# Two-layer decoder with selective scans: convolution taps made by TensorE from diagonals, and a 3 MB load placed behind row loads

## The chip, the core and the metric

The kernel runs on one core of a Trainium2 chip. A core has five engines that run their own instruction queues in order and meet through semaphores: TensorE (PE; its weight loads are listed as PEld), VectorE (DVE), ScalarE (ACT), GpSimd (POOL) and SyncE (SP). DMAs are issued here from the queues of SP and ACT. On-chip data lies in SBUF (128 partitions); matmuls write to PSUM. The metric is the device time of one execution in microseconds (us), lower is better. One execution is also profiled; the times within the kernel are from that one.

## The reference

The input `x` is 4 batches of 256 tokens by 256 channels; `ctx_1024` is 4 x 256 x 128. Six steps follow one another, each added to `x`:

```
x = x + L0_attn(layernorm(x))                 # 8 heads of 32, 2 kv heads, window of 64
x = x + L0_xattn(ctx, z=layernorm(x))         # selective scan over ctx, gated by z
x = x + L0_ffn(layernorm(x))                  # 704 wide
x = x + L1_attn(layernorm(x))                 # 16 heads of 128, 4 kv heads, causal
x = x + L1_xattn(ctx, z=layernorm(x))         # selective scan again, other weights
x = x + L1_ffn(layernorm(x))                  # 32 experts, 6 per token, and a shared one
```

The selective scan, cut to what matters (256 inner channels `e`, 16 states `n`, 4 taps):

```
x  = in_proj_w @ ctx                          # 256 x 128
xc = causal depthwise conv(x, conv_w)         # 4 taps per channel
u  = silu(xc + conv_b)
dt_low, B, C = split(x_proj_w @ u)
dt = softplus(dt_proj_w @ dt_low + dt_proj_b)
state = state * exp(dt * A) + (dt * u) * B    # per token, channel and state
y = sum over n of state * C + D * u;  result = y * silu(z)
```

The scan reads only `ctx`, so it doesn't depend on `x`; the gate does.

## The kernel before

All arithmetic is in fp32, with few exceptions. `x` stays in SBUF. The work is one long program for all four batches; a scheduler in the language's layer decides, at build time, in which order each engine issues its instructions, from the order of the program text, the dependences and a cost model. At run time that order is fixed on each engine.

**The folded convolution.** Projection and convolution are one: for each tap `k`, `taps[:, k, :]` is `in_proj_w` (transposed, 128 x 256) times tap `k` of each channel, and four matmuls per half of the channels (L165), each on `ctx` shifted by one token, add up in PSUM. `taps` must hold the tap of channel `e` in column `e` on all 128 partitions. To get that, the kernel before copies `conv_w` from `params` to a row `cw` in device memory (L287, four loads in elements of 4 bytes, two for each layer), then broadcasts `cw` to all partitions (L290, issued on ACT's queue) and multiplies by `inproj` (L294; on DVE for layer 0, on POOL for layer 1). The tiles `inproj`, `taps`, `xproj` and `dtproj` are shared by both layers.

**The scan.** `mamba_front(l, bp, pool)` makes `u`, `dt`, `du` and writes the rows of B and C to device memory (`bc`, L180) for two batches at a time. `mamba_scan` then runs over the states: for each state and half of the channels it broadcasts one row of B (`bt`) and one of C (`ct`) to all partitions (L208, 256 KB each, on SP's queue, three buffers each), ACT makes `h` (L214), POOL makes `db` (L216), DVE scans (L217) and multiplies by `ct` into `hc` (L219); `hc` is added up by PE (L234) or POOL (L236). It is a generator: `run(s00, 4)` takes it four steps on (two states a step), so that scan and attention are interleaved in the program text.

**The first attention.** `head0(b)` normalizes and transposes a batch (L135, L139, L142), projects it (L337) and applies the rotation (`r`, `rr`, L347, L348) and the normalization with its rsqrt steps (L103 to L110) on DVE, up to `qn`, `krep` and `vn`; `tail0(b)` does scores, softmax and output and adds to `x` (L479). `far` (L319) is made of the constants `cst`. The order in the text: the front of the first two batches, `head0(0)`, `head0(1)`, and then for each `b`: four steps of scan `s00`, `head0(b + 2)`, `tail0(b)`, two more steps; after `tail0(0)` the front of the other two batches.

**The second attention's projections.** `wqkv1` (3 MB) is loaded on SP's queue (L492) after that block. For the layer norm of the queries and keys the mean of each head is taken out of the weights: `wmean` by a reduction and a scaling on DVE (L498, L499), then two subtractions on POOL (L501). Nothing holds these in their place but the data, so the scheduler puts the load right behind the first loads, and `wmean` and the subtractions before the first scan.

Then come the first FFN (gates, L530 to L562, with the rest of the scan and the fronts of layer 1), the second attention with the layer 1 scans, and the experts.

## Time and profile before

| | |
|---|---|
| median of 5 runs | 962.02 us (954.41 to 966.72) |
| the profiled execution | 963.15 us, its span 961.3 us |
| mean granted TensorE clock | 0.923 |
| busy, share of the span | PE 85%, DVE 68%, ACT 50%, POOL 53%, PEld 53% |
| HBM read | 71.58 MB, 76 GB/s over the span |
| first convolution matmul | at 30.75 us |
| first scan | at 60.45 us |
| first addition of attention to `x` | at 111.50 us |
| experts, PE full | from about 720 us to the end |

How to read it: the span runs from the first to the last instruction of the profiled execution; its own time has a few us around that. A line of a timeline gives start, duration, engine, line of the program, operation, output and inputs, a count, and in brackets how long the engine was idle before and what ended that. `SPq` and `ACTq` are the queues in which DMAs are issued. PEclk is the clock granted to TensorE, in tenths or as a share of full speed; a matmul of fp32 operands has two records.

### The profile page before, as it was taken

The numbers are of one execution on the slowest core, as the hardware profiler recorded it, in microseconds if no ns is written. First come the engines' busy times: TensorE is split into PE (matmuls) and PEld (weight loads), VectorE is DVE, ScalarE is ACT, GpSimd is POOL, SyncE is SP. The second block draws the span as 40 slices with busy tenths as digits, with TensorE's granted clock in tenths as the row PEclk, the third lists the DMA queues.
The fourth block names the chain that finished last, engine by engine and source line by source line (L and its number), as shares of the span: only waits on it lengthen the run. The fifth ranks groups of instructions, "written<-read, shape, count | busy, mean of one in ns | idle before, by whom it ended". The sixth has DMA issues, their size and how long they took to land. (4 is left out here: it accounts for less than half of the span.)

```text
span 961.3 us, 10234 instructions
## 1 busy us (share of the span) xinstructions
PE 821.5 (85%) x2986; PEld 508.9 (53%) x2986; DVE 650.0 (68%) x1230; ACT 481.1 (50%) x1187; POOL 505.9 (53%) x493
## 2 busy tenths in 40 slices
PE   0649799996996979879887988897879999999997
PEld 0226466752442435545554656465556666666665
DVE  1499976647886739998779989796225555555554
ACT  1345676647968826746684776557433111111110
POOL 2175656638667753885756698383123333333334
PEclk9979878957995979989989999899979999999999
DMA  7245443636561220121111112000030101111101
GB/s 199 110 148 163 120 152 124 207 91 214 191 200 44 76 99 1 55 77 34 55 33 55 45 48 76 10 12 1 0 111 1 44 23 45 26 40 45 44 0 44
DMA packets 38071, 73.54 MB, mean 77 GB/s; under 512 B 6512, under 2 KB 9472, under 8 KB 37760
## 3 DMA queue, kind: packets, MB, share of 16 engines
q1 hardware_dynamic: 36016, 69.92, 22.9%
q10 hardware_dynamic: 2000, 2.99, 0.9%
q8 instruction: 23, 0.38, 0.2%
q14 instruction: 32, 0.26, 0.1%
HBM read 71.58 MB, written 1.32 MB: 76 GB/s over the span
## 5 line engine op out<-in xcount | busy, mean ns | idle before, releaser
L216 POOL TENSOR_TENSOR db<-bt,du 128x512 f32<-128x512 f32 x128 | 163.8, 1289 | 80.8 <-DVE h L217 67.8
L980 DVE SCALAR_TENSOR_TENSOR acc<-ps,gate,acc 128x256 f32<-128x256 f32 x256 | 111.3, 479 | 109.3 <-PE ps L971 109.3
L217 DVE TENSOR_TENSOR_SCAN h<-h,db 128x512 f32<-128x512 f32 x128 | 153.3, 1215 | 20.1 <-ACT h L214 16.5
L945 POOL TENSOR_TENSOR hT<-hr 128x512 f32<-128x512 f32 x68 | 70.8, 1042 | 166.5 <-ACT hr L943 166.5
L943 ACT ACTIVATE hr<-ph 128x512 f32<-128x512 f32 x68 | 40.6, 598 | 181.6 <-PE ph L935 179.4
L971 PE MATMUL ps<-w,hT 128*128 128x256 f32 x512 | 120.6, 379 | 0.0
L935 PE MATMUL ph<-moe_xnT,w 128*128 128x512 f32 x256 | 120.1, 592 | 0.0
L971 PEld LDWEIGHTS ps<-w,hT 128*128 128x128 f32 x512 | 97.3, 190 | 39.7 <-issue 29.7
L619 PE MATMUL ps<-wqkv,xnT 128*128 128x512 f32 x192 | 102.8, 654 | 11.8 <-ACT sq L634 5.3
L214 ACT ACTIVATE h<-dt,negA 128x512 f32<-128x512 f32 x128 | 86.3, 688 | 52.5 <-DVE hc L219 50.1
L219 DVE TENSOR_TENSOR hc<-h,ct 128x512 f32<-128x512 f32 x128 | 85.2, 680 | 2.2
L226 POOL TENSOR_TENSOR y<-y,hc 128x512 f32<-128x512 f32 x64 | 83.1, 1305 | 5.3 <-DVE hc L219 5.1
L612 POOL TENSOR_TENSOR rq<-rq,nhalf 128x8 f32<-128x8 f32 x20 | 35.5, 1775 | 62.4 <-DVE rq L611 62.4
L746 POOL TENSOR_TENSOR sc<-sc,rsum 128x512 f32<-128x512 f32 (+1 forms) x32 | 46.6, 1476 | 41.2 <-DVE rsum L744 40.9
L935 PEld LDWEIGHTS ph<-moe_xnT,w 128*128 128x128 f32 x256 | 48.6, 190 | 34.3 <-issue 31.1
L741 ACT ACTIVATE sc<-sc,nm 128x128 f32<-128x128 f32 (+1 forms) x128 | 56.8, 450 | 17.2 <-DVE nm L736 14.7
L634 ACT ACTIVATE sq<-ps 128x128 f32<-128x128 f32 x160 | 42.7, 281 | 36.9 <-PE ps L619 33.3
L619 PEld LDWEIGHTS ps<-wqkv,xnT 128*128 128x128 f32 x192 | 36.5, 208 | 42.1 <-issue 28.2
L784 PE MATMUL ps<-wo,oT 128*128 128x256 f32 x256 | 57.0, 381 | 1.1 <-ACT oT L777 1.1
L234 PE MATMUL ps<-hc,ident 128*128 128x512 f32 x64 | 41.9, 744 | 17.1 <-DVE hc L219 17.1
L784 PEld LDWEIGHTS ps<-wo,oT 128*128 128x128 f32 x256 | 48.1, 190 | 9.7 <-ACT oT L777 3.3
L165 PE MATMUL ps<-ctxT,taps 128*128 128x512 f32 x64 | 36.9, 696 | 11.4 <-DVE taps L294 11.4
(198 smaller groups left out, 1524.8 us busy)
## 6 DMA issues: line engine op xcount, KB each, us to landing
bt<-bc SPq DMA_DIRECT2D x96, 256.0 KB, 3.3
ct<-bc SPq DMA_DIRECT2D x96, 256.0 KB, 3.5
w<-in_w_dram SPq DMA_DIRECT2D x16, 512.0 KB, 3.6
wqkv<-in_wqkv_dram SPq DMA_DIRECT2D x1, 3072.0 KB, 14.8
wo<-in_wo_dram SPq DMA_DIRECT2D x1, 2048.0 KB, 7.6
x<-in_x_dram SPq DMA_DIRECT2D x4, 256.0 KB, 5.0
taps<-cw ACTq DMA_DIRECT2D x2, 512.0 KB, 9.2
out_dram<-acc SPq DMA_DIRECT2D x4, 256.0 KB, 2.2
```

Source lines behind the costliest of these rows:

```text
L214: nc.scalar.activation(h, dt[:, c, :], AF.Exp, scale=negA[:, a : a + 1])
L216: nc.gpsimd.tensor_mul(db, bt, du[:, c, :])
L217: nc.vector.tensor_tensor_scan(h, h, db, 0.0, ALU.mult, ALU.add)
L219: nc.vector.tensor_mul(hc, h, ct)
L226: nc.gpsimd.tensor_add(y[:, c, :], y[:, c, :], state(n, c, bt, ct))
L619: mm(pq, lhsT=xnT[:, f, c * P : (c + 1) * P], rhs=wqkv1[:, f, ch * 512 : (ch + 1) * 512], start=(f == 0), stop=(f == 1),)
L741: nc.scalar.activation(part, part, AF.Exp, bias=nm[:, qc, j : j + 1], accum_out=rsum[:, qc, j : j + 1])
L784: mm(pout[:, c * 256 : (c + 1) * 256], lhsT=oTs[h // 4][:, h % 4, c * P : (c + 1) * P], rhs=wo1[:, 8 * gp + h, :], start=(h == 0), stop=(h ...
L935: mm(ph_, lhsT=w1[:, f, :], rhs=xnT[:, f, hf * 512 : (hf + 1) * 512], start=(f == 0), stop=(f == 1),)
L945: nc.gpsimd.tensor_mul(hT, hr, hr)
L971: mm(po[:, t * 256 : (t + 1) * 256], lhsT=hT[:, tl * P : (tl + 1) * P], rhs=w2, start=True, stop=True,)
L980: nc.vector.scalar_tensor_tensor(acc[:, tl, :], po[:, t * 256 : (t + 1) * 256], gate[:, tl, e : e + 1], acc[:, tl, :], ALU.mult, ALU.add,)
```

## The change

The taps are made on chip. `conv_taps(l)` multiplies the identity by the tap columns of `params` (`par`, already in SBUF, one value per partition, tap and half) into four times two 128 x 128 diagonals `diag`; a matmul with a matrix of ones then yields, on every partition, the row of taps (two matmuls of 512 columns); DVE multiplies each from PSUM by `inproj`. For layer 0 it is called ahead of the first front, for layer 1 at the start of the first FFN. The loads of `cw`, its copies in device memory and the broadcasts go; `inproj`, `taps`, `xproj` and `dtproj` now have one tile for each layer, so that layer 1's loads needn't wait for layer 0's use. PSUM for the matmuls comes from the pool `pf`, one buffer, that the fronts use as well.

The load of `wqkv1` moves into the loop, behind the first batch's steps, and is held on SP's queue behind the last row load traced so far (the `ct` of state 12, first half of the channels). This is an order of issue, not a wait for that row to land. `wmean` and the subtractions follow in the text as before; what they read lands later.

The rest of the text is the same. In the built order of instructions the engines differ from before up to the middle of the first FFN, and from there to the end they are the same; ACT's order has 62 table loads where before it had 70.

```diff
@@ mamba_scan
-            nc.sync.dma_start(out=t_, in_=bc[r : r + 1, :].to_broadcast([P, 512]))
+            loads.append(nc.sync.dma_start(out=t_, in_=bc[r : r + 1, :].to_broadcast([P, 512])).ins)
@@ per layer l
-        inproj = mp.tile([P, 256], F32, name="inproj")
-        taps = mp.tile([P, 4, 256], F32, name="taps")
-        xproj = mp.tile([P, 2, 40], F32, name="xproj")
-        dtproj = mp.tile([8, 256], F32, name="dtproj")
+        inproj = mp.tile([P, 256], F32, name=f"inproj{l}")
+        xproj = mp.tile([P, 2, 40], F32, name=f"xproj{l}")
+        dtproj = mp.tile([8, 256], F32, name=f"dtproj{l}")
         nc.scalar.dma_start(out=inproj, in_=i_)
-        cw = dpool.tile([1, 8 * P], F32, name=f"cw{l}")
-        for c in range(2):
-            w = l * M_COLS + M_CONVW + 4 * c
-            nc.sync.dma_start(
-                out=cw.rearrange("o (k c p) -> (o p) c k", k=4, c=2)[:, c, :], in_=params[:, w : w + 4]
-            )
-        nc.scalar.dma_start(out=taps.rearrange("p k e -> p (k e)"), in_=cw.to_broadcast([P, 8 * P]))
         nc.scalar.dma_start(out=xproj, in_=x_)
         nc.scalar.dma_start(out=dtproj, in_=d_)
-        (nc.vector if l == 0 else nc.gpsimd).tensor_mul(
-            taps, taps, inproj.unsqueeze(1).to_broadcast([P, 4, 256])
-        )
-        mw.append((taps, xproj, dtproj))
+        mw.append([inproj, xproj, dtproj])
+    ones = mp.tile([P, P], F32, name="ones")
+    nc.gpsimd.memset(ones, 1.0)
+    def conv_taps(l):
+        diag = mp.tile([P, 4, 2, P], F32, tag="diag", name="diag")
+        taps = mp.tile([P, 4, 256], F32, name=f"taps{l}")
+        w = par[:, l * M_COLS + M_CONVW : l * M_COLS + M_CONVW + 8].rearrange("p (c k) -> p k c", k=4)
+        nc.vector.tensor_mul(
+            diag,
+            ident.unsqueeze(1).unsqueeze(1).to_broadcast([P, 4, 2, P]),
+            w.unsqueeze(3).to_broadcast([P, 4, 2, P]),
+        )
+        for k in range(0, 4, 2):
+            pw = ps(pf)
+            mm(pw, lhsT=ones, rhs=diag[:, k : k + 2].rearrange("p k c e -> p (k c e)"), start=True, stop=True)
+            nc.vector.tensor_mul(
+                taps[:, k : k + 2, :],
+                pw.rearrange("p (k e) -> p k e", k=2),
+                mw[l][0].unsqueeze(1).to_broadcast([P, 2, 256]),
+            )
+        mw[l][0] = taps
@@ first attention
+        conv_taps(0)
         s00 = mamba_scan(mamba_front(0, 0, pf), psd, psy)
         parts = [head0(0), head0(1)]
         for b in range(B):
...
             run(s00, 2)
-    nc.sync.dma_start(out=wqkv1, in_=wqkv1_in)
+            if b == 0:
+                with tc.issue_after(loads[-1]):
+                    nc.sync.dma_start(out=wqkv1, in_=wqkv1_in)
@@ first FFN
+        conv_taps(1)
         scans = []
```

## The prediction

> **What bounds the kernel now.** I read first the busy shares in 40 slices, then the waits of the first 62 us, then that stretch in order of time, then busy time by stage. The slices (24.0 us each) show where no engine is busy:

> ```profile
> PE   0649799996996979879887988897879999999997
> DVE  1499976647886739998779989796225555555554
> POOL 2175656638667753885756698383123333333334
> PEclk9979878957995979989989999899979999999999
> ```

> The first slice is empty on all engines. From slice 30 on PE is full (the experts); before that the bound changes by stage. Who waited in the first 62 us:

> ```profile
> POOL wqkv L501 <- DVE wmean L499: 31.5, 1, 31.5
> DVE taps L294 <- DMA taps<-cw: 14.9, 1, 14.9
> PE ps L165 <- DVE taps L294: 11.4, 1, 11.4
> ACT xn L135 <- issue: 9.1, 1, 9.1
> ```

> So the first convolution waits for `taps`, and `taps` for a load. In order of time:

> ```profile
> 3.48 5.02 SPq L287 DMA_DIRECT2D cw<-in_params_dram  x4
> 16.32 0.34 ACTq L290 DMA_DIRECT2D taps<-cw  x1
> 17.50 0.60 ACT L135 ACTIVATE xn<-x,ln_nb,ln_rs 128x256 f32<-128x256 f32 x1 [9.15 <-issue]
> 29.47 1.22 DVE L294 TENSOR_TENSOR taps<-taps,inproj 128x1024 f32<-128x1024 f32 x1 [14.87 <-DMA taps<-cw]
> 30.75 5.80 PE L165 MATMUL ps<-ctxT,taps 128*128 128x512 f32 x8 [11.42 <-DVE taps L294]
> 37.87 0.49 DVE L347 TENSOR_TENSOR r<-ps,cst 128x320 f32<-128x320 f32 x1 [7.18 <-PE ps L337]
> 38.68 5.48 DVE L498 TENSOR_REDUCE wmean<-wqkv 128x40 f32<-128x5120 f32 x1
> 45.12 10.15 POOL L501 TENSOR_TENSOR wqkv<-wqkv,wmean 128x2560 f32<-128x2560 f32 x2 [31.54 <-DVE wmean L499]
> 46.90 4.05 DVE L361 SCALAR_TENSOR_TENSOR r<-a_mean,r 128x768 f32<-128x768 f32 x1
> 50.87 4.95 DVE L192 TENSOR_TENSOR du<-dt,u 128x512 f32<-128x512 f32 x1
> 60.45 1.22 DVE L217 TENSOR_TENSOR_SCAN h<-h,db 128x512 f32<-128x512 f32 x1
> ```

> The 4-byte loads of `cw` land at 16.3; only then can ACT's queue issue the broadcast of `taps`, with `xn` behind it, and that lands at 29.4, beside the 3 MB of `wqkv1` issued at 14.19. Then `wmean` and its subtraction stand ahead of the first scan (L217). By stage:

> ```profile
> core 0: us, PE busy (x) PEld busy (x) DVE busy (x) ACT busy (x) POOL busy (x), PEclk, DMA share, GB/s
> 60.45:111.50 51.05, 40.74 (x172) 24.26 (x170) 49.42 (x87) 31.74 (x60) 30.09 (x27) 0.93 0.48 146
> 111.50:217.10 105.60, 102.15 (x392) 67.14 (x393) 70.72 (x111) 65.35 (x123) 58.85 (x53) 0.76 0.44 141
> 217.10:300.00 82.90, 63.15 (x168) 28.54 (x166) 62.63 (x107) 64.20 (x79) 57.54 (x68) 0.86 0.53 175
> ```

> From the first scan to the first attention result added to `x` (111.5) DVE is full; from there to the fourth (217.1) PE is, at a granted clock of 0.76; then ACT leads with 77%, PE and DVE a point or two below it.

> **The head.** Gone are four `cw` loads, the broadcast and its wait. New for layer 0: `diag` (one 128x1024 multiply, 1.22 by the old `taps` row), two fp32 128x512 matmuls (two records each; eight took 5.80 at the first convolution, so 1.45 a matmul) and two multiplies from PSUM (0.68, the DVE rows of 128x512). `par` lands at 6.4 (issued 1.41, 5.0 to landing); DVE is free of the layer norm's sums at 9.6, so `diag` ends at 10.8, the first matmul at 12.3, the first multiply near 13. In the changed kernel's instruction order PE does the transposes of `xn` before the second matmul. `xn` needs POOL's power (ends 13.58 before; nothing here moves that), so two `xn` end at 14.8, transposes at 15.4, second matmul 16.9, second multiply 17.6. The first projection follows the second matmul (two records, 1.45): `r` at 18.4 against 37.87, 19.5 earlier; the convolution at 18.4 against 30.75, 12.3 earlier. `xn`'s 9.15 us of waiting behind the DMA goes; what is late next is that power on POOL.

> **From there to the first scan.** `wmean` (5.48 + 0.17) and what the two DVE rows above took over the same rows later (4.05 - 0.95 and 4.95 - 0.68, together 7.37) leave: 13.0. Not all counts, for the chain convolution, `u`, `xdbl`, `bc`, first row takes as long as before: from 30.75 to 50.0 (47.0 issued, 3.0 to landing) 19.3. 18.4 + 19.3 + 1.3 (`db`) = 39.0, against 60.45: 21.4. By then DVE has also finished the first head's rsqrt, `qn` and the next `r`, some 3.3 us which before came after the first scan, and DVE is full from there to 111.5. I take **25** at the first addition to `x`. Bounds: 12.3 (the convolution's start alone) and 32.5 (19.5 + 13.0).

> **What is paid back.** The load is issued behind the row `ct` of state 12, and in the changed order `wmean` stands just after the first addition to `x`, its scaling nine scans later, the two subtractions on POOL beside that.
> - `wmean`, 5.65 on DVE. It now lies where DVE is busy 67%: 3.8. Bounds 0 and 5.65.
> - The subtractions, 10.15 on POOL. POOL has three `db` made ahead when it comes to them, so `db` is covered; DVE's two-operand work behind them is not. Before, they held DVE 7.37: I take 7.4. Bounds 0 and 10.15.
> - 3 MB beside row loads, which now queue behind it on SP. The nearest row: 2.3 MB of FFN weights issued from 215.4 to 217.2, and row loads issued from 217.24 on landed within 5.3 us against 3.3. Three row buffers at 3.9 us a scan (51.05 over 13) hide that; 1. Bounds 0 and 11.5 (14.8 landing, less 3.3). DVE reaches `wmean` some 27 us after the load's slot by the times of before (91.0 to 118.1), so it should have landed.
> - The second layer's taps: 2 matmuls, 2 multiplies; its `diag` lies in the head while DVE waits. Gone: a POOL multiply of 2.35 that waited 4.61. 0; bounds -2 and 3.

> Together 12.2.

> **ACT tables.** The changed ACT stream has eight table loads fewer (1.28 each), five of them after the last attention of layer 0, where ACT is busy 77%: 6.4 x 0.77 = 5 gained. Bounds 0 and 10.2. From the second half of the FFN on the order of all engines is as before, so what is won at 300 us stays.

> Sum: -25 + 12.2 - 5 = -17.8. The profiled execution took 963.15 (span 961.3 and 1.85 around it): **945**. That execution is 1.1 above the median of 962.02.

> [...] While the subtractions ran, one DVE multiply took 4.95 instead of 0.68. [...]

> **Rivals.**
> - *The payback is hidden.* Where PE is full at 111 to 217, DVE and POOL have room: nothing paid but 1, and all tables gained: -25 + 1 - 10.2 = -34, 929. For it: DVE 67%, POOL 56%. Against it: DVE issues in order, and attention waits on it.
> - *It is paid in full.* 5.65 + 10.15 + 7.37, and no tables: -25 + 23.2 = -2, 961. For it: that is what these steps cost before.
> - *The clock falls (slower).* 111.5 to 217.1 holds 102.15 us of PE at 0.76, 77.6 at full clock. New gaps on PE while DVE does `wmean` may keep it at half clock as from 188.6 to 212.5. At a mean of 0.55 the stage takes 141, 35 more: -17.8 + 35.5 = +18, 981. It decides below 0.65 (119.4, +14).
> - *The head isn't freed.* `far`, ahead of the first multiply on DVE, waits for `cst`, which landed at 13.9; if x and `cst` come later still, only the 12.3 remains, less 12.2: no change, 963.

> **Chances.** Forecast 0.45 (its own range 935 to 953), hidden 0.18, in full 0.20, clock 0.12, head 0.05. A measurement of this kernel tells about 1% (9.6 us; its five runs spread from 954.41 to 966.72). Faster: 0.18, 0.43 of the forecast, and 0.09 of the middle cases: 0.70. Slower: the clock case, 0.11. Within: 0.19. The range leaves out the clock case and the far end of the hidden one: 929 to 965.

> **What would show it.** First `r` near 18 and first scan near 39; the first addition to `x` near 86; DVE idle less than 3 us before `wmean`; rows landing under 6 us beside the load; the granted clock of the attention stage at 0.7 or above; and the second half of the FFN some 18 us earlier, with equal stage lengths after. Wrong would be: a wait for `cst`, a wait of DVE for `wqkv1`, POOL's `db` late behind the subtractions, or a slower clock.

## The result, and the profile after it

The changed kernel took 967.41 us (median of 45 runs, 959.04 to 971.17) against 964.88 us for the kernel before on the same chips (87 runs, 954.41 to 975.11): a ratio of 1.0025 with a 95% interval of 1.0012 to 1.0038. The forecast of 945 is missed, and so is its range, which ended at 965. The ratios, here and below, leave out executions more than 1.5% above the fastest of their kernel, as runs of a slower state; with them e7 would stand at 0.974, e9 at 0.980, e11 at 0.987, e6 and e8 at 0.998, and no conclusion changes. The profiled execution of the changed kernel took 970.52, with a span of 968.6 at a mean granted clock of 0.899; before it was 963.15, 961.3 and 0.923.

The same four rows of the 40 slices, now of the changed kernel (24.2 us each):

```profile
PE   4898997988977969879888989898879999999997
DVE  3888659567886739998778989796124555555554
POOL 3355449366676754785766798384123333333333
PEclk9978556797996979899989999899969999999999
```

The first slice is no longer empty: PE goes from 0 to 4, DVE from 1 to 3. But the granted clock in slices 5 and 6 (97 to 145 us) is 0.5, with PE at 0.9 and 0.9 busy; before, two slices had 0.5 as well (9 and 13), but not side by side.

Who waited in the first 62 us of the changed kernel (us in total, times, longest), of that list the rows that bear on the taps:

```profile
PE ps L303 <- DVE diag L296: 11.1, 1, 11.1
DVE r L358 <- PE ps L348: 6.3, 2, 3.8
DVE taps L304 <- PE ps L303: 4.6, 2, 3.9
```

The waits for the `taps` load (14.9 and 11.4) and POOL's 31.5 for `wmean` are gone; PE's wait for `diag` is from the start of the program, while nothing else is there for it to do. In order of time on DVE:

```profile
13.14 0.69 DVE L304 TENSOR_TENSOR taps<-ps,inproj 128x512 f32<-128x512 f32 x1 [0.73 <-PE ps L303]
17.74 0.69 DVE L304 TENSOR_TENSOR taps<-ps,inproj 128x512 f32<-128x512 f32 x1 [3.92 <-PE ps L303]
19.65 0.49 DVE L358 TENSOR_TENSOR r<-ps,cst 128x320 f32<-128x320 f32 x1
39.14 1.22 DVE L217 TENSOR_TENSOR_SCAN h<-h,db 128x512 f32<-128x512 f32 x1
...
88.13 0.67 DVE L490 TENSOR_TENSOR x<-x,ps 128x512 f32<-128x512 f32 x1
...
93.23 5.45 DVE L513 TENSOR_REDUCE wmean<-wqkv 128x40 f32<-128x5120 f32 x1
```

The first scan starts at 39.14 (60.45 before), the first addition to `x` is at 88.13 (111.50), and `wmean` follows 5 us later without waiting for its load. By stage (first row: from the start to the gate of the FFN's second half, then the three stages between first scan, first addition, fourth addition and that gate):

```profile
core 0: us, PE busy (x) PEld busy (x) DVE busy (x) ACT busy (x) POOL busy (x), PEclk, DMA share, GB/s
0.00:287.13 287.13, 245.42 (x775) 138.30 (x776) 208.81 (x321) 159.04 (x263) 160.17 (x168) 0.80 0.47 156
39.14:88.13 48.99, 45.11 (x168) 26.31 (x167) 43.50 (x75) 32.03 (x58) 27.40 (x25) 0.86 0.59 197
88.13:206.60 118.47, 109.11 (x371) 72.03 (x372) 83.31 (x110) 54.31 (x112) 65.45 (x53) 0.64 0.39 127
206.60:287.13 80.53, 66.37 (x171) 28.69 (x171) 62.35 (x86) 55.52 (x68) 56.51 (x57) 0.92 0.56 193
```

The same first row of the kernel before:

```profile
0.00:286.25 286.25, 224.11 (x769) 128.22 (x769) 202.89 (x316) 166.84 (x271) 162.20 (x168) 0.87 0.50 161
```

These two rows hold the whole answer in short. The gate of the FFN's second half comes at 287.13 instead of 286.25. PE was idle for 62.1 us before (286.25 - 224.11) and for 41.7 after (287.13 - 245.42): the change removed 20.4 us of idle time. And PE was busy for 21.3 us more. Of these, 7.1 us are new work, the eight records of L303 (taps). The other 14 us are the matmuls of before, done at a lower mean clock (0.80 against 0.87). (No clock is on record before 18.8 us, or 35.0 in the kernel before; all means count that stretch as full. PE is busy for some 6 us of it in both.)

Where the lead went, in us by which the changed kernel is ahead:

| milestone | before | after | ahead |
|---|---|---|---|
| first scan | 60.45 | 39.14 | 21.3 |
| addition to `x`, batch 0 | 111.50 | 88.13 | 23.4 |
| batch 1 | 157.69 | 148.88 | 8.8 |
| batch 2 | 183.65 | 187.73 | -4.1 |
| batch 3 | 215.34 | 206.60 | 8.7 |
| first gate of the FFN's second half | 286.25 | 287.13 | -0.9 |

What PE did in the stretch in which the lead went, from the changed kernel's timeline:

```profile
98.54 0.59 PE L428 MATMUL ps<-qkT 32*128 32x192 f32 x2
...
109.32 1.00 PE L428 MATMUL ps<-qkT 32*128 32x192 f32 x2
...
112.69 1.91 PE L234 MATMUL ps<-hc,ident 128*128 128x512 f32 x2
...
143.65 3.78 PE L482 MATMUL ps<-wo,attnT 128*128 128x256 f32 x8
```

The same pair of score matmuls (L428) takes 0.59 at 98.5 and 1.00 at 109.3. Between the two, at 100.7, the granted clock had gone to 0.50, and it stayed there for 47.8 us; it came back at 148.5, after the eight 128-row matmuls of L482 and the pair of L234 behind them. The row of that stretch:

```profile
100.70:148.50 47.80, 46.52 (x136) 31.91 (x136) 28.84 (x41) 20.87 (x49) 23.98 (x17) 0.50 0.35 111
```

PE was busy for 46.52 of the 47.80 us. So a busy PE, as the profile counts busy (the ends of its matmuls are modelled), did not bring the clock back. Two of DVE's waits in that stretch show who sets the pace:

```profile
114.71 0.69 DVE L238 TENSOR_TENSOR y<-y,ps 128x512 f32<-128x512 f32 x1 [7.05 <-PE ps L234]
...
137.23 0.21 DVE L461 RECIPROCAL rden<-ps 128x8 f32<-128x8 f32 x1 [7.38 <-PE ps L459]
```

Behind each of them, in DVE's order, stands a scan (at 115.32 and 137.39).

In the first 360 us of the profiled executions the clock is at half for 105.8 us before and for 143.4 after.

### The profile page after: what moved, and what is told of

Read it like the earlier page. It is cut to its first block, busy times and chain, and to the rows that moved or that the text cites. A ratio compares the mean times of both kernels' runs of the same rounds, so it can differ in the third digit from the quotient of the medians.

```text
span 968.6 us, 10230 instructions
## 1 busy us (share of the span) xinstructions
PE 847.9 (88%) x2994; PEld 522.3 (54%) x2994; DVE 654.9 (68%) x1235; ACT 472.4 (49%) x1179; POOL 504.4 (52%) x493
## 5 line engine op out<-in xcount | busy, mean ns | idle before, releaser
L996 DVE SCALAR_TENSOR_TENSOR acc<-ps,gate,acc 128x256 f32<-128x256 f32 x256 | 111.3, 479 | 109.3 <-PE ps L987 109.3
L217 DVE TENSOR_TENSOR_SCAN h<-h,db 128x512 f32<-128x512 f32 x128 | 153.7, 1217 | 24.9 <-ACT h L214 21.5
L961 POOL TENSOR_TENSOR hT<-hr 128x512 f32<-128x512 f32 x68 | 70.8, 1041 | 170.2 <-ACT hr L959 170.2
L214 ACT ACTIVATE h<-dt,negA 128x512 f32<-128x512 f32 x128 | 86.7, 689 | 68.6 <-DVE hc L219 68.3
L628 POOL TENSOR_TENSOR rq<-rq,nhalf 128x8 f32<-128x8 f32 x20 | 35.5, 1774 | 59.9 <-DVE rq L627 59.7
L234 PE MATMUL ps<-hc,ident 128*128 128x512 f32 x64 | 46.2, 815 | 9.7 <-DVE hc L219 9.7
L738 PE MATMUL ps<-kT,qT 128*128 128x256 f32 x128 | 37.0, 415 | 11.1 <-DVE sc L731 9.0
```

Of the source, the lines that this page charges most:

```text
L214: nc.scalar.activation(h, dt[:, c, :], AF.Exp, scale=negA[:, a : a + 1])
L217: nc.vector.tensor_tensor_scan(h, h, db, 0.0, ALU.mult, ALU.add)
L961: nc.gpsimd.tensor_mul(hT, hr, hr)
L996: nc.vector.scalar_tensor_tensor(acc[:, tl, :], po[:, t * 256 : (t + 1) * 256], gate[:, tl, e : e + 1], acc[:, tl, :], ALU.mult, ALU.add,)
```

## The experiments

In what follows a matmul is called dense when it runs over 128 rows with some hundred columns or more, and thin when it has 32 rows (the scores) or 33 columns (softmax times values). The first theory was the clock: the second layer's convolution, made of dense matmuls, had moved out of the attention stage, which kept mostly thin ones. There were two rivals: the moved work (`wmean` and the subtractions now stand in that stage), and the end of layer 0's scans as the gate of all that follows. A mean clock over the span splits every profiled execution in two: span times clock is what it would take at full clock, if everything followed PE's clock, and the rest is lost to the clock. The table has all kernels; the ratio is over a kernel's runs, while span, clock and the columns behind them are of one profiled execution each, and "half" is the time at half clock in its first 360 us. "Rows" are those over which the score matmuls run.

| kernel | ratio to before (95%) | span | clock | span x clock | lost | half |
|---|---|---|---|---|---|---|
| before | 1 | 961.3 | 0.923 | 887.3 | 74.0 | 105.8 |
| after | 1.0025 (1.0012-1.0038) | 968.6 | 0.899 | 870.8 | 97.8 | 143.4 |
| e1 taps only | 1.0019 (0.9991-1.0047) | 960.5 | 0.914 | 877.9 | 82.6 | 122.9 |
| e2 load only | 1.0234 (1.0199-1.0269) | 981.9 | 0.895 | 878.8 | 103.1 | 147.3 |
| e3 second taps early | 0.9962 (0.9937-0.9987) | 956.5 | 0.912 | 872.3 | 84.2 | 126.3 |
| e4 after + 64 dense | 0.9927 (0.9898-0.9955) | 958.9 | 0.921 | 883.1 | 75.8 | 99.0 |
| e5 before + 64 dense | 1.0123 (1.0094-1.0152) | 975.8 | 0.929 | 906.5 | 69.3 | 88.4 |
| e6 after + 64 thin | 0.9959 (0.9928-0.9990) | - | - | - | - | - |
| e7 early + 64 dense | 0.9706 (0.9668-0.9744) | 935.9 | 0.934 | 874.1 | 61.8 | 81.9 |
| e8 load only + 64 dense | 0.9950 (0.9917-0.9983) | 963.2 | 0.921 | 887.1 | 76.1 | 102.4 |
| e9 after, 128 rows | 0.9787 (0.9725-0.9849) | 937.6 | 0.937 | 878.5 | 59.1 | 88.7 |
| e10 before, 128 rows | 0.9762 (0.9714-0.9809) | 941.1 | 0.941 | 885.6 | 55.5 | 68.3 |
| e11 early + 64 thin | 0.9829 (0.9755-0.9904) | 949.4 | 0.915 | 868.7 | 80.7 | 116.1 |
| e12 early, 128 rows | 0.9730 (0.9683-0.9777) | 936.5 | 0.934 | 874.7 | 61.8 | 81.9 |
| e13 taps only, 128 rows | 0.9706 (0.9674-0.9737) | 938.0 | 0.932 | 874.2 | 63.8 | 81.9 |
| e14 load only, 128 rows | 0.9897 (0.9865-0.9929) | 956.4 | 0.926 | 885.6 | 70.8 | 88.7 |
| e15 early + 32 dense | 0.9952 (0.9922-0.9982) | 960.5 | 0.916 | 879.8 | 80.7 | 116.1 |
| e16 as e7, load in its old place | 1.0056 (1.0026-1.0086) | 968.2 | 0.915 | 885.9 | 82.3 | 122.9 |
| e17 after, 64 rows | 0.9881 (0.9853-0.9910) | 951.2 | 0.922 | 877.0 | 74.2 | 95.6 |

That the split means something is shown by the changed kernel itself. Over 46 executions of this one program the mean clock ran from 0.897 to 0.912, and the time with it: 0.93 us for each us lost to the clock (correlation 0.95), from 959.04 at 0.911 to 971.17 at 0.899. In most other kernels the slope was lower (0.64 over 91 executions of the kernel before, 0.62 in e3, 0.69 in e9, 0.90 in e4), so the split overstates what the clock costs where PE does not set the pace.

### One part of the change at a time

```diff
-            if b == 0:
-                with tc.issue_after(loads[-1]):
-                    nc.sync.dma_start(out=wqkv1, in_=wqkv1_in)
+    nc.sync.dma_start(out=wqkv1, in_=wqkv1_in)
```

(behind the loop over `b`, where the kernel before has it)

> The changed kernel with the 3 MB load back where it stood before (issued after the last attention batch is put in order), so only the taps change. Clock theory (thin matmuls alone let the clock fall in the attention stage once the second layer's convolution left it): that convolution stands early on PE again (positions 160 to 227 of PE's order), so the mean granted clock from the first to the fourth addition to x is back at 0.72 or more, against 0.64 in the changed kernel and 0.76 before, and the kernel is 10 to 20 us faster than before. Moved-work theory (wmean and the subtractions in the attention stage cost the gain): they now stand in the head, the first scan is near 48 instead of 39, and the kernel is 8 to 13 us faster than before. Scan-end theory (the second half of the FFN waits for the end of layer 0's scans, which did not come earlier): within 4 us of before, with the gate of the FFN's second half at 286 to 288 again.

Measured 1.0019: the scan-end theory's number, with the gate of the FFN's second half at 284.16. The clock of the stage from the first to the fourth addition was 0.73, as the clock theory asked, and yet the gain did not come: the first scan was 11.6 us earlier (48.89), the lead was still 13.9 us at the 31st scan, and it was lost from 157.1 on, where the clock was at half for 27.3 us.

```diff
+            if b == 0:
+                with tc.issue_after(loads[-1]):
+                    nc.sync.dma_start(out=wqkv1, in_=wqkv1_in)
-    nc.sync.dma_start(out=wqkv1, in_=wqkv1_in)
```

(in the kernel of before, with this alone)

> The kernel of before with only the 3 MB load moved behind the row load of the 13th state; the taps are made as before. Clock theory: the second layer's convolution stays early on PE (positions 141 to 200), so the clock of the attention stage stays at 0.72 or more, and the head loses its wmean (5.65) and the subtractions beside it: 5 to 12 us faster than before. Moved-work theory: the head gains about 13, the stage pays it back and more, and the kernel is the same to 8 us slower than before, with the stage from the first to the fourth addition 8 to 13 us longer at an unchanged clock. Scan-end theory: within 4 us of before.

Measured 1.0234, far beyond all three. The first theory in its narrow form falls here: the second layer's convolution stood early on PE, and the clock fell all the same, to 147.3 us of half clock. The first scan was 13.2 us earlier (47.23), but between the 7th and the 10th scan 24 us were lost. Two stretches of that kernel's windows, and what DVE did in them:

```profile
70.00:80.00 10.00, 10.00 (x29) 6.41 (x28) 8.11 (x11) 3.58 (x10) 6.80 (x5) 0.50 0.74 243
80.00:90.00 10.00, 10.00 (x37) 8.25 (x38) 2.98 (x12) 4.20 (x9) 2.35 (x1) 0.50 0.02 8
```

```profile
86.67 0.21 DVE L450 RECIPROCAL rden<-ps 128x8 f32<-128x8 f32 x1 [8.13 <-PE ps L448]
```

PE is busy for every one of these 20 us, at 0.50, and DVE waits 8.13 us for it: `rden` stands ahead of the next scan on DVE (at 98.36), in the order written, so a slow PE stops the scans too.

```diff
         conv_taps(0)
+        conv_taps(1)
...
-        conv_taps(1)
```

(in the changed kernel, from behind the FFN's weights to here)

> The changed kernel with the second layer's taps made right behind the first layer's, so that its convolution stands early on PE (positions 145 to 196). Clock theory: the mean granted clock from the first to the fourth addition to x is 0.72 or more and the kernel is 8 to 18 us faster than the changed one. Moved-work theory: the wmean and the subtractions stay in the stage, so the same as the changed kernel within 4 us. Scan-end theory: the stage may be shorter, but the second half of the FFN starts within 3 us of 287 and the kernel is within 4 us of the changed one.

Measured 0.9962, some 6 us faster than the changed kernel (8.8 by the medians, on different chips). The clock of the stage was 0.76 and half clock fell by 17 us, to 126.3. That is a little less than the 8 to 18 us of the clock theory, and more than the moved-work theory allowed; the gate of the FFN's second half came at 281.01, which the scan-end theory had excluded. So the second layer's late convolution looks like one cause of the lower clock, and not the only one; the order of other instructions changed as well.

### Dense matmuls that compute nothing

```diff
                     psc = ps(pb)
+                    for _ in range(2):
+                        mm(psc, lhsT=identb, rhs=warm, start=True, stop=True)
```

(in the changed kernel, two ahead of each group of scores of layer 0's attention, 64 in all; the scores overwrite what they give)

> [...] Clock theory: the granted clock of the attention stage rises to 0.8 or more, the stage is no longer than the changed kernel's 118.5 us although it holds more work, and the kernel is 0 to 15 us faster than the changed one. Moved-work theory (the clock is only a symptom of gaps that DVE makes): the clock may rise, yet the stage keeps its length and the kernel is within 4 us or, as PE has more to do, up to 14 us slower. Scan-end theory: the gate of the FFN's second half stays within 3 us of 287.

Measured 0.9927: some 9.5 us faster than the changed kernel, though the 64 extra matmuls kept PE busy for 23.6 us. The clock of the stage rose from 0.64 to 0.82 and the stage fell from 118.5 to 114.0 us. The gate of the FFN's second half came at 276.42, against the scan-end theory once more. The 14 us by which the moved-work theory let it be slower was the author's estimate for these matmuls, which no run shows; shown are the 23.6 us. A gain from added work speaks for the clock; but the extra instructions also moved others, so one run alone does not show it.

The same matmuls in the kernel of before (e5), and in that kernel with the load moved (e8):

> The kernel of before with two extra dense 128x512 bf16 matmuls ahead of each group of scores (64 in all; in the changed kernel they took 23.6 us of PE). If the clock alone made the changed kernel with them faster, the kernel of before gains as much from them: 6 to 12 us faster than before, half clock up to 360 us falling from 105.8 to below 95. If they only keep up what the change would otherwise lose, they are worth nothing or cost here: 0 to 10 us slower than before, half clock up to 360 us about as before.

Measured 1.0123, 12 us slower (half clock 88.4). In the kernel of before the 17 us less of half clock are worth some 9 us at most, and the matmuls cost more. They pay only where the clock is low.

> The kernel of before with only the 3 MB load moved, and the 64 dense matmuls. If the 22 us that the moved load alone cost are the clock's (half clock up to 360 us was 147.3 against 105.8), most of them go: within 6 us of before, half clock below 110. If they are the price of the moved work itself (wmean and the subtractions in the attention stage), they stay: 15 us or more slower than before.

Measured 0.9950, as the clock theory had it: with the dense matmuls the 22 us that the moved load had cost are gone (half clock 102.4 in place of 147.3). The order of the other instructions moved as well.

> The changed kernel with the same 64 extra matmuls, each with 32 rows in place of 128 (the same 512 columns, so by estimate the same time on PE). If it is the dense work that brings the clock back, these do nothing for it: half clock up to 360 us at 140 or more and 8 to 25 us slower than the changed kernel. If it is only that PE is kept busy, as fast as with the dense ones: 6 to 12 us faster than the changed kernel, half clock near 100.

(In e4's order, with `identb[hp, :]` and `warm[hp, :]`.) Measured 0.9959: some 6 us faster than the changed kernel, which is what was expected if it were only that PE is kept busy, and not the 8 to 25 us slower of the other side. The interval overlaps that of e4. The table has no split for it; over ten of its runs, from 956.44 at a clock of 0.921 to 968.15 at 0.904, the mean lost to the clock is 82.9, against 72.6 over e4's twelve. The clock is lower with thin matmuls, then, but most of that did not show in the time. As a test of rows it is inconclusive.

> The changed kernel with the second layer's taps made early and the 64 dense matmuls as well. Clock theory: the two remedies overlap, half clock up to 360 us at 95 or below, and the kernel is 8 to 16 us faster than before. If PE's own work is the bound once the clock is up, the 23.6 us of extra matmuls eat the rest: within 4 us of the version with the early taps alone (0.9962 of before).

(e3 and e4 together.) Measured 0.9706, some 28 us faster than before, more than either theory expected: of the kernels that compute the whole of the reference it is the fastest, ahead of both that were compared.

### The same order, another number of rows

What was missing was an edit that changes the clock and nothing else. The scores of a head are matmuls over 32 rows (L428 and L429). Over all 128 rows they compute something else (sums over four heads), but every engine keeps its instructions in their order, and PE streams the same columns.

```diff
-                    mm(psc[:, 0:NEAR], lhsT=qkT[hp, 2 + g, 0:P], rhs=qkT[hp, g, 0:NEAR], start=False, stop=False)
+                    mm(psc[:, 0:NEAR], lhsT=qkT[0:P, 2 + g, 0:P], rhs=qkT[0:P, g, 0:NEAR], start=False, stop=False)
```

(and the same for the second of them).

> The changed kernel whose score matmuls run over all 128 rows of queries and keys in place of the 32 of their head, so that each score is summed over four heads (another computation); every engine has the same instructions in the same order as the changed kernel. Clock theory: half clock up to 360 us falls from 143.4 to 100 or below and the kernel is 10 to 20 us faster than the changed one. Order theory (the time follows where the instructions stand, the clock is a by-product): within 4 us of the changed kernel.

> The kernel of before with the same change of the score matmuls, again in its own order. Clock theory: it loses less by the clock to begin with (105.8 us of half clock up to 360 us), so it gains 0 to 8 us, and the changed kernel with full rows is 8 to 20 us faster than this one: what was forecast for the change comes out once the clock is held up in both. Order theory: within 4 us of before, and of the changed kernel with full rows.

> The changed kernel with early taps of the second layer, score matmuls over all 128 rows (sums over four heads), in its own order. Clock theory: half clock up to 360 us falls from 126.3 to 95 or below and it is 6 to 16 us faster than with 32 rows (0.9962 of before). Order theory: within 4 us of that.

Measured 0.9787, 0.9762 and 0.9730: each gains 22 to 23 us (with intervals of 3 to 6 us either way) over the same kernel with 32 rows (1.0025, 1, 0.9962), where 10 to 20 were expected of e9 and 6 to 16 of e12. The stage of the changed kernel (first to fourth addition) with 128 rows, to be laid beside the row 88.13:206.60 above:

```profile
85.45:184.68 99.23, 83.28 (x371) 61.61 (x372) 83.17 (x110) 53.83 (x112) 65.33 (x53) 0.81 0.49 152
```

The same 371 matmul records in 83.28 us of PE instead of 109.11; DVE's, POOL's and ACT's busy times are equal to within 0.5 us; the stage is 19.2 us shorter. Some of it is not the clock: with 128 rows the pair of L428 takes 0.49 at full clock instead of 0.59, 3.2 us over 32 pairs.

```profile
94.03 0.49 PE L428 MATMUL ps<-qkT 128*128 128x192 f32 x2
```

The rest is the clock. The order and the other engines' work are unchanged, and every other shape of matmul takes the same time in both kernels at the same granted clock: a record of L234, for instance, has a median of 592 ns at full clock and 1,061 at half in both, one of L458 277 and 402. Only how many of them ran at half differs.

The other half of the expectation fell. The kernel of before was to gain 0 to 8 us and gained 23. Its stage, at 32 rows and at 128:

```profile
111.50:215.34 103.84, 101.13 (x386) 66.36 (x386) 68.96 (x109) 63.60 (x121) 58.53 (x53) 0.75 0.44 143
```

```profile
112.10:195.61 83.51, 77.87 (x386) 54.70 (x386) 68.75 (x109) 62.39 (x119) 57.37 (x52) 0.90 0.54 171
```

It, too, had been held by the clock (0.75, now 0.90). With 128 rows in both, the two kernels are equal within their intervals. But their clocks are still not: 0.90 against 0.81 in the stage, 68.3 against 88.7 us of half clock. And beside the clock the stage holds 14.4 us more of DVE in the changed kernel (83.17 against 68.75): `wmean` is 5.6 of it, the second layer's taps 1.4, and 9.6 are the rsqrt steps (L107 to L110), as many as before but slower, most of that beside the subtractions on POOL; a `du` fewer takes 1.5 off. The lead of 26.7 us at the first addition (112.10 to 85.45) is 10.9 at the fourth and 1.2 at the gate of the FFN's second half.

The same pair for the fastest version, whose 64 dense matmuls were cut to 32 rows:

```diff
-                        mm(psc, lhsT=identb, rhs=warm, start=True, stop=True)
+                        mm(psc, lhsT=identb[hp, :], rhs=warm[hp, :], start=True, stop=True)
```

> The fastest version so far (second layer's taps early, 64 dense matmuls) with the 64 matmuls cut to 32 rows; the same order on every engine. Clock theory: half clock up to 360 us rises from 81.9 to 115 or more and the kernel is 10 to 20 us slower than with the dense ones (ratio to before 0.98 to 0.992). Order theory: the gain came from another order of instructions, so within 4 us of 0.9706 of before.

Measured 0.9829 against 0.9706, 12 us, as expected of the clock. The attention stage of e7 and then of e11:

```profile
85.39:188.66 103.27, 98.94 (x433) 61.45 (x432) 78.58 (x113) 58.31 (x118) 69.05 (x56) 0.85 0.48 154
```

```profile
84.31:202.03 117.72, 110.79 (x433) 70.94 (x432) 78.78 (x113) 58.08 (x118) 69.26 (x56) 0.71 0.42 136
```

The same records on every engine, 14 us apart, and only PE's busy time and clock differ. Of the 25 us by which e7 is faster than e3, though, only these 12 are shown to be the clock's: e11, with thin matmuls, is already 13 us faster than e3, which has none, and those two differ in order.

And the changed kernel with the scores over 64 rows, two heads:

```diff
-                    hp = slice(32 * j, 32 * j + 32)
+                    hp = slice(64 * (j // 2), 64 * (j // 2) + 64)
```

> The changed kernel whose score matmuls run over 64 rows in place of 32 (each score is summed over two heads), again in the changed kernel's own order. If the clock follows the columns weighted by rows, this lies between 32 and 128 rows: half clock up to 360 us at 100 to 130 (143.4 and 88.7 at the ends) and 5 to 15 us faster than the changed kernel. If anything below 128 rows counts as thin: half clock at 135 or more and within 4 us of the changed kernel. If 64 is as good as 128: half clock below 95 and 17 to 22 us faster.

Measured 0.9881, 14 us faster than with 32 rows and 9 slower than with 128: the number of rows counts. Its half clock (95.6) is nearer to the 128-row end than expected.

### Which part brings the low clock

The taps alone (e1) and the load alone (e2), with 128 rows and otherwise in their own orders:

> Only the taps changed (the 3 MB load in its old place), score matmuls over all 128 rows (sums over four heads). If the moved load is what eats the gain, this is 8 to 14 us faster than the kernel of before with full rows (0.9762 of before): 0.962 to 0.968. If the taps' place eats it, or the scans end when they end anyhow: within 4 us of 0.976.

> Only the 3 MB load moved, taps as before, score matmuls over all 128 rows. With the old 32 rows it cost 22.6 us. If that was the clock's: within 5 us of 0.9762 of before. If it is the price of wmean and the subtractions in the attention stage: 8 us or more slower, 0.985 or above.

Measured 0.9706 and 0.9897. The first lies between its two expectations; the second is the number that was expected if the moved work itself has the price, and not the clock. With 128 rows the four corners are 0.9762 (neither), 0.9706 (taps), 0.9897 (load), 0.9787 (both): the taps gain 5 to 11 us, the moved load costs 8 to 13, each with an interval of some 5 us either way. The split says what of this is the clock's. Here it is the mean over the runs behind the ratios, each of which has its span and clock on record, because single executions scatter (the clocks of e9 go from 0.922 to 0.937, and its profiled execution is the one with 0.937):

| against the kernel without the change, us | span x clock | lost |
|---|---|---|
| taps alone, 32 rows / 128 rows | -8.3 / -12.6 | +7.3 / +7.9 |
| load alone, 32 rows / 128 rows | -6.3 / +1.0 | +26.5 / +12.9 |
| both, 32 rows / 128 rows | -16.0 / -8.8 | +17.4 / +11.1 |

(Each mean is known to some 1 us, those of e9 to 3.) By this split neither part costs anything at full clock, and each is bought with a lower clock, the load with the most. So the load's price in e14 is read as the clock's too, though its expectation had called that number the price of the moved work; that rests on the split alone.

Two more from e7: the load back in its old place, and one dense matmul in place of two (`range(1)`).

> As the version with early taps and two dense matmuls, but the 3 MB load in its old place, with wmean and the subtractions in the head. If the place of the load costs nothing once the clock is held: first scan some 8 us later, time within 5 us of 0.9706 of before. If the load behind the first scan is worth its 8 us: 6 to 12 us slower. If wmean in the attention stage costs more than it saves in the head: 4 to 10 us faster.

Measured 1.0056, 34 us slower than e7; the expected 6 to 12 is far off. The first scan came at 58.2 (42.5 in e7, so 16 us later and not 8), and half clock was 122.9. With the load in its old place the subtractions stand ahead of the scan again; and the new order, with the same dense matmuls, holds the clock far worse.

> The changed kernel with the second layer's taps early and one dense matmul ahead of each group of scores in place of two (32, by estimate some 12 us of PE). If two are more than the clock needs, 0 to 8 us faster than with two (0.9706 of before); if the clock follows their number, half clock up to 360 us rises from 81.9 to 95 or more and it is 4 to 12 us slower.

Measured 0.9952, 24 us slower than with two, and no faster than with none (0.9962). Half clock was 116.1; 44.4 us of it in one stretch from 136.7 on. From none to one to two, then, the gain did not follow the number of dense matmuls.

## Why the prediction was wrong, step by step

**The head was right.** `diag` was ready at 10.9 (10.8 forecast), the multiplies at 13.14 and 17.74 (near 13 and 17.6), `r` at 19.65 (18.4), the first scan at 39.14 (39.0), the first addition at 88.13 (near 86): a lead of 23.4 where 25 was taken.

**What is paid back, item by item.** `wmean` took 5.45 and did not wait for its load, which was issued at 77.10. The row loads behind that load were slower than allowed: the first landed after 10.96 us, the next four, issued from 86.5 to 87.9, after 5.7 to 6.2, and the write of `bc` just ahead of them after 10.81, where the prediction asked for less than 6. (Its row for this, "issued from 217.24 on", was not the nearest: the first of those loads whose landing is on record was issued at 222.38, five us behind the weights.) Still no engine waited for a row, as the waits from 77 to 125 us name no DMA, so the 1 us taken was enough. The subtractions took 8.92 on POOL in place of 10.15, and what they cost DVE can be read beside them. First POOL, then DVE:

```profile
143.24 4.46 POOL L516 TENSOR_TENSOR wqkv<-wqkv,wmean 128x2560 f32<-128x2560 f32 x1
...
148.89 4.46 POOL L516 TENSOR_TENSOR wqkv<-wqkv,wmean 128x2560 f32<-128x2560 f32 x1
```

```profile
144.81 2.93 DVE L108 TENSOR_TENSOR rs_t<-rs_t,a_rs 128x24 f32<-128x24 f32 x1
...
149.48 3.92 DVE L110 TENSOR_TENSOR rs_r<-rs_r,rs_t 128x24 f32<-128x24 f32 x1
```

Two DVE multiplies of 24 elements, 0.18 each at 31 us with POOL idle, last until the POOL instruction beside them ends (147.74 against 147.70, 153.40 against 153.35): 6.5 us lost, 7.4 taken. When DVE came to them, 2.89 us were left of the first POOL instruction and 3.87 of the second: the price of these two multiplies is what was left, and not the whole 8.92.

**ACT's tables:** eight loads fewer, as forecast (62 against 70). ACT was busy for 159.04 of 287.13 us, and in the stage where the 5 us were to come, from the fourth addition to the gate, for 55.52 of 80.53; that stage became 9.6 us longer, so the 5 us don't show.

**The second layer's taps** were put at 0. The PE records of both layers' taps took 7.1 us, and the second layer's, 3.1 of them, stand in the attention stage. Their place was worth 6 us more (e3): an order that moved a dense step was costed as if only the step's own length mattered.

**The step that failed is the sum over the attention stage,** which carried the stage on at its old clock of 0.76 and so put the clock's change at nothing. It was listed as a rival with 0.12: "the clock falls", deciding below 0.65, 119.4 us long. Measured: 0.64, and 118.5 us long. That estimate of the length was right; the chance given to it was not. The reason given for it, gaps while DVE does `wmean`, was wrong: over the 47.8 us at half clock PE was busy for 46.5. The trace of the kernel before had such a stretch too, from 195 to 210 us:

```profile
195.00:210.00 15.00, 15.00 (x41) 9.15 (x41) 6.07 (x10) 5.50 (x9) 5.52 (x5) 0.50 0.29 85
```

Up to the gate, by the split above, the clock cost 18.8 us more than before. Stage by stage, after less before in the profiled executions (the prediction ended the attention stage at 217.1, which is the first gate; the fourth addition stands at 215.34):

| stage | forecast | measured | of it at full clock | lost to the clock |
|---|---|---|---|---|
| start to first scan | -21.4 | -21.3 | -17.9 | -3.4 |
| to the first addition | -3.6 | -2.1 | -5.4 | +3.4 |
| to the fourth addition | +12.2 | +14.6 | -2.4 | +17.1 |
| to the gate of the FFN's second half | -5 | +9.6 | +7.9 | +1.7 |
| sum | -17.8 | +0.9 | -17.9 | +18.8 |

That the sum at full clock comes out at the forecast is luck, as two of its terms miss and cancel. The 12.2 paid back on DVE and POOL in the attention stage are not there at full clock, as the rival "the payback is hidden" had it; the +14.6, close to +12.2, comes from the clock. And the stage behind it, forecast 5 us shorter, is longer at nearly the same clock (0.92 against 0.93). By the means over all runs the whole kernels stand 16.0 us apart at full clock, with 128 rows 8.8; how much of the forecast would have come at an equal clock is known no better than that.

**The gate.** "What is won at 300 us stays" was right in the order, but the second half of the FFN waits for layer 0's scans, and these had lost their lead by then: the 7th scan was 24.1 us ahead, the 17th 7.4, the 28th 3.8, the 34th 4.9 behind and the last of layer 0, the 64th, 1.4 behind. On DVE they stand behind `rden`, `y` and `x`, which wait for PE. But the clock is not all of it. The stage from the fourth addition to the gate, in the kernel before and in the changed kernel with 128 rows:

```profile
215.34:286.25 70.91, 58.56 (x161) 27.48 (x161) 56.41 (x82) 55.02 (x67) 52.94 (x54) 0.93 0.61 204
```

```profile
184.68:265.25 80.57, 66.06 (x171) 28.30 (x171) 62.13 (x86) 55.52 (x68) 56.45 (x57) 0.91 0.57 194
```

It takes 80.5, 80.6 and 80.4 us in the three kernels with the changed kernel's order (32, 128 and 64 rows), whatever the clock of the stage ahead (0.64, 0.81, 0.76), and 70.9 in both with the order of before. So most of these 9.6 us (7.9 at full clock) belong to the order: more is left to do in that stage (5.9 us more of DVE, 7.8 of PE, the first front of the second layer among it). Which of it sets the length is open. In the profiled execution what follows the FFN's last addition took 6.5 us more (628.0 against 621.5), with 54.2 against 44.3 us of half clock after 360 us; the medians differ by 2.5 only.

**What stays open:** why two dense matmuls with the early taps are so much better than with the load in its old place. Of the 34 us between e7 and e16, the means over their runs put 26 down to the clock (lost 55.0 against 80.9) and 9 not; the two have different orders, so why the clock holds in one is not shown.

## What to carry to other kernels

Where a stage is bound by PE and its granted clock is below 1, the clock is a term of the sum (here the stage from the first to the fourth addition took 118.5 us at 0.64 and 99.2 at 0.81, with the same order on every engine): give the stage's PE time at full clock, and ask of every edit what it does to the mix of dense and thin matmuls there, not only what it costs. An edit that keeps every engine's order (here: the number of rows) separates the clock from the schedule; an added or moved instruction does not. And work freed at the start of a program reaches its end only if the stage behind it can go faster (here a lead of 23.4 us at the first addition was 0.9 behind at the gate): read first what sets that stage's pace.

## What the runs showed of the hardware

In the traces of the two compared kernels the granted clock is 1.00 or 0.50 and changes on a grid of 3.41 us: its stretches last 3.4, 6.8, 10.2, 13.7 us and so on, all 66 that end within a trace a whole number of such intervals. I counted, in the first 350 us of the profiles of both kernels and of all seventeen experiments, what PE streamed in each such interval: the columns of its matmuls, each weighted by its share of the 128 rows, and what clock the next interval got.

```
clock now   weighted columns   intervals   next at full   next at half
half        over 1600          202         163             39
half        up to 1600         367           4            363
full        over 1600         1043        1013             30
full        up to 1600         162          18            144
```

A busy PE was not enough for full clock: PE was busy for 46.5 of 47.8 us at a clock of 0.50, and of 332 intervals at half clock in which it was busy for over 97%, 188 were followed by another at half. In these records the next clock went with how many columns were streamed and over how many rows (95% of the intervals by the table).
